# Second cross attention of a perceiver kernel: the two score passes one after the other, a quarter of the side matrix added by TensorE, value sums kept in a bank of PSUM

## The chip, the cores and the metric

The kernel runs on one core of a Trainium2 chip. The metric is the device time of one execution in microseconds; the time before is the median of three runs. The engines named here are TensorE (PE, with PEld for its weight loads), VectorE (DVE), ScalarE (ACT), GpSimd (POOL) and SyncE (SP). PSUM, which TensorE writes, has eight banks of 128 partitions by 512 float32.

## The reference, cut to what matters

A latent `x` of 128 rows by 256 passes through four layers. Each has a cross attention over a context of 12544 rows, a self-attention and a feed-forward part. The change is in the cross attention of the second layer (`l1x` in the kernel), with 16 heads of 16 features and a side matrix:

```python
K = (K_in @ Wk + bk).reshape(b, l, NH, DK).transpose(0, 2, 1, 3)
V = (V_in @ Wv + bv).reshape(b, l, NH, DK).transpose(0, 2, 1, 3)
Q = (Q_in @ Wq + bq).reshape(b, lp, NH, DK).transpose(0, 2, 1, 3)
KQ = jnp.einsum('bhld,bhpd->bhlp', K, Q) / np.float32(np.sqrt(DK))
KQ = KQ + mask_pad.reshape(b, 1, l, 1)
KQ = KQ + mask_attn.T.reshape(1, 1, l, lp)
alpha = jax.nn.softmax(KQ, axis=2)
O = jnp.einsum('bhlp,bhld->bhpd', alpha, V)
O = O.transpose(0, 2, 1, 3).reshape(b, lp, NH * DK)
return O @ Wo + bo
```

`K_in` and `V_in` are the context, `Q_in` the normalized latent, `mask_pad` a vector over the 12544 keys and `mask_attn` the side matrix, 128 by 12544. The softmax runs over the keys, with the same side matrix for all heads.

## The kernel before

**Stages.** The twelve parts run in order. Each cross attention needs keys and values of the whole context. These projections are cut into jobs (`project`, L199): for each of 25 chunks of 512 keys two key jobs (`K`, `k`, one for each half of the heads, L221) and two value jobs (`V`, `W`, L241), 99 for one attention. Each result goes to DRAM and is read back later. All jobs of all four attentions stand in one list, `self.jobs`, in order. They are taken from its head in three ways. `pump` in a cross attention's loop takes as many as `quota` says (L716); in the second attention one in three ticks of four. `one` (L155) takes one job ahead of every bank that a self-attention or feed-forward part asks for. `need` (L176) takes as many as it must until certain jobs are done, and so forces them where a load depends on them. A key job writes a staging tile `kst` of two parts, high and low, of which there are two buffers, and GpSimd's queue stores it; context chunks come through three buffers `ctx` on SyncE's queue.

**Two passes.** `cross` (L383) computes the scores twice. The first pass has queries on partitions and keys along the row, and finds the largest score of each query. The second pass has keys on partitions, 128 at a time, and queries of four heads along the row; it subtracts the maximum through an extra product, and its exponentials are the weights of the value product. Scores have a contraction of 32 rows (16 features in two parts, high and low), so four row tiles of TensorE work at once, each with a bank of its own. Four heads make a group (`G`), four groups one attention.

**Ticks.** A block is 2048 keys, 512 for each row tile; the last block has two row tiles of 128 keys. `ticks` (L446) holds for each group six blocks of four pieces and one short piece, 100 in all. The loop (L703) makes 127 turns: turn n runs the first pass of piece n and the second pass of piece n-27, because a group's second pass needs its maxima. So 27 turns hold first passes alone, 73 hold both, 27 hold second passes alone. The order of the instructions is written by hand (`manual_schedule`), and every engine runs its own list in that order.

**One turn.** `scores` (L587) takes two banks for the first pass of rows 2 and 3, four for the second pass and two more for the first pass of rows 0 and 1: all eight, from a ring of eight. It issues the products of both passes interleaved: rows 2 and 3 begin with the first pass while rows 0 and 1 begin with the second. VectorE then finds the maxima of rows 2 and 3 (`largest`, L553), adds the side matrix for the second pass (`exps`, L572) row by row, each followed by ScalarE's exponential, and finds the maxima of rows 0 and 1. In `largest` one instruction adds the side tile and takes the maximum (L562). Then the loop pumps a job, and `values` (L652) multiplies the exponentials of the turn before with the values into a new bank and VectorE adds that to an accumulator in SBUF (`acc`, L675).

**Loads.** `load_first(n+2)` (L461) and `load_second` (L481) issue their loads on SyncE's queue two turns ahead. The side tiles of the first pass (`f`, L475) are four for a block, from six buffers, so that two of a new block wait until two of the old are given back. The side tiles of the second pass (`ft`, L500) are one load of 256 KB for a piece, all four row tiles in it, from a transposed copy `fsideT`.

Of the kernel before, what the change touches and what calls it, by code (L numbers as in the profile page):

```python
# [10 lines left out]
F32 = mybir.dt.float32  # L11
# [8 lines left out]
P = 128  # L20
# [50 lines left out]
def _block(b):  # L71

    return (4, SEG) if b < NB - 1 else (2, P)
# [21 lines left out]
class Net:  # L95
    def __init__(self, ctx, tc, io):
# [7 lines left out]
        self.dp = ctx.enter_context(tc.tile_pool(name="scratch", bufs=1, space=DRAM))  # L104
        self.ps1 = ctx.enter_context(tc.tile_pool(name="ps1", bufs=8, space=PSUM))

# [55 lines left out]

    def bank(self, name):
        return self.ps1.tile([P, 512], F32, name=name, tag="one")

# [15 lines left out]
    def projections(self, names):  # L181
        self.kx, self.vx = {}, {}
        for l, name in enumerate(CROSS):
            if name not in names:
                continue
            gw = 17 * GROUP[name]
            for b in range(NB):
                ns, seg = _block(b)
                self.kx[name, b] = self.dp.tile([16, 32 * ns, seg], F32, name=f"{name}_kx{b}",
                                                tag=f"{name}_kx{b}")  # L190
                self.vx[name, b] = self.dp.tile([272 // gw, P, ns * seg // P, gw], F32,
                                                name=f"{name}_vx{b}", tag=f"{name}_vx{b}")
            if l == 0:
                passes = ["KVW", "k"]
            else:
                passes = ["KkVW"]
            self.project(name, passes)

    def project(self, name, passes):  # L199
# [183 lines left out]
    def cross(self, name, side=False, project=True, quota=None):  # L383
# [6 lines left out]
        with ExitStack() as es:  # L390
# [28 lines left out]
            def queries(g):  # L419

                q = qp.tile([P, 2, G, P], F32, name=f"{name}_q{g}", tag="q")
                qf = qp.tile([P, G, P], F32, name=f"{name}_qf{g}", tag="qf", bufs=1)
                wq = wqs.pop(g)
# [12 lines left out]

            kt, vt, ft, neg, qs, mxs, acc, wqs = {}, {}, {}, {}, {}, {}, {}, {}
            loaded = {"s": -1, "v": -1, "f": -1, "t": -1}
# [42 lines left out]
            def load_second(n):  # L481

                while loaded["v"] < min(n, len(ticks) - 1):
# [15 lines left out]
                    if side:  # L499
                        t = ep.tile([P, 4, P], F32, name=f"{name}_g{g}_{b}_{u}", tag="ft", bufs=3)  # L500
                        at = b * BK // P + u * 4
                        nc.sync.dma_start(out=t[:, :ns, :],
                                          in_=self.io["fsideT"][:, at : at + ns, :])
                        ft["t", g, b, u] = t

            def score_banks(n, kind, half):
# [4 lines left out]
            def first_ops(n, banks, t):  # L511
# [17 lines left out]
                return ops  # L529

            def second_ops(n, banks, t):

# [4 lines left out]
                for a in range(na):  # L537
                    at = (u * na + a) * P
                    for h in range(0, G, 2):
                        c = (a * G + h) * P  # L540
                        lhs = (mrow[r, b * SEG + at : b * SEG + at + P] if masked
                               else self.units[r, :])
                        ops.append((banks[t][:, c : c + 2 * P], r32(lhs),
                                    r32(neg[g][r, h : h + 2].rearrange("p h q -> p (h q)")),
                                    True, False))
                        for i in range(2):
# [25 lines left out]
            def exps(n, e, banks):  # L572
# [3 lines left out]
                for t, bank in banks.items():  # L576
                    src = bank[:, :m]
                    if side:
                        nc.vector.tensor_tensor(  # L579
                            out=e[:, t, :m].rearrange("p (h q) -> p h q", h=G),  # L580
                            in0=src.rearrange("p (h q) -> p h q", h=G),
                            in1=ft["t", g, b, u][:, t, :].unsqueeze(1).to_broadcast([P, G, P]),
                            op=ALU.add)
                        src = e[:, t, :m]
                    nc.scalar.activation(e[:, t, :m], src, AF.Exp)  # L585

            def scores(n, m):  # L587
# [37 lines left out]
                return (m, e) if second else None  # L625

            def lower(g):

# [23 lines left out]
            def values(part):  # L652
# [4 lines left out]
                na = min(4 // G, seg // P)  # L657
                ps = self.bank(f"{name}_av{n}")
                for t in range(ns):
                    for a in range(na):  # L660
                        for h in range(G):
# [3 lines left out]
                                             vt[g, b][:, at : at + 32],  # L665
                                             e[:, t, c * P : (c + 1) * P], start=(t == 0),
                                             stop=(t == ns - 1), skip_group_check=True)
                used = 32 * na * G
                first = b == 0 and u == 0
                if first:  # L670
                    acc[g] = self.small.tile([P, P], F32, name=f"{name}_acc{g}", tag="acc")
                if first:
                    nc.vector.tensor_copy(acc[g], ps[:, :P])
# [25 lines left out]
            pending = None  # L699
            load_queries(0)  # L700
            with tc.manual_schedule():
                qs[0] = queries(0)
                for n in range(len(ticks) + lag):  # L703
                    load_first(n + 2)
                    if n >= lag - 2:
                        load_second(n - lag + 2)
                    new = scores(n if n < len(ticks) else None, n - lag if n >= lag else None)
                    if n < len(ticks) and n % per == per - 1:
# [5 lines left out]
                    if n % per == 2 * per // 3 and n // per + 1 < 16 // G:  # L714
                        qs[n // per + 1] = queries(n // per + 1)
                    self.pump(quota(n, len(ticks), lag))  # L716
                    if n >= lag:
# [5 lines left out]
                values(pending)  # L723
                finish(16 // G - 1)

            nc.vector.tensor_tensor(out=o, in0=o, in1=self.row(f"{name}_vb"), op=ALU.add)
# [885 lines left out]
```

## Time and profile before

| What | us |
|---|---|
| Median of three runs (2648.64 to 2659.61) | 2657.65 |
| Profiled execution | 2661.88 |
| Its span, first to last instruction | 2660.1 |
| TensorE busy (matmul) | 2412.7 (91%) |
| VectorE busy | 1719.1 (65%) |
| ScalarE busy | 1229.3 (46%) |
| GpSimd busy | 419.6 (16%) |
| First score product of the second attention | 770.1 |
| First product of its second pass | 938.8 |
| Last first-pass product | 1361.8 |
| Last value product | 1471.4 |
| L562, add and maximum, 416 times | 254.3 busy |
| L579, side matrix added for the second pass, 392 times | 243.3 busy |
| L585, the exponentials of it, 392 times | 234.0 busy |
| L675, sums of the values, 96 times | 27.1 busy |

The page gives for each engine its busy time, a strip of 40 equal slices with the busy share in tenths, and groups of instructions by line. A group's line has the engine, the operation, output and inputs by the program's names with shapes, the number, then busy time, mean duration in ns, and the idle time of the engine just before, with what ended it. A line with "us, times, longest" is a wait: who waited for whom. In a timeline the columns are start, duration, engine, line, operation, output and inputs, and the number of instructions drawn together. Matmuls are pipelined, so a busy TensorE is not TensorE at its peak: the distance between starts says more.

### The profile page before, as it was taken

How to read it: one execution, taken by the hardware profiler on the slowest of the kernel's cores; microseconds unless marked ns; L12 is line 12 of the kernel's file. 1: busy time of each engine (PE TensorE's matmuls, PEld its weight loads, DVE VectorE, ACT ScalarE, POOL GpSimd, SP SyncE). 2: the span in 40 equal slices, each digit the busy share in tenths (PEclk: the TensorE clock that was granted, in tenths of full speed). 3: DMA queues.
4: the chain of work that ended last, by engine and by line, in shares of the span. 5: the costliest groups of instructions: out<-in, count | busy, mean ns of one | idle time of the engine just before them, and what ended most of it. 6: DMA issues, size and time to landing. Idle time of an engine off the chain costs nothing. (4 is left out here: it accounts for less than half of the span.)

```text
span 2660.1 us, 94232 instructions
## 1 busy us (share of the span) xinstructions
PE 2412.7 (91%) x41075; PEld 1874.3 (70%) x41075; DVE 1719.1 (65%) x3814; ACT 1229.3 (46%) x2256; POOL 419.6 (16%) x803
## 2 busy tenths in 40 slices
PE   7789989999968799999999898799999949999969
PEld 5567668886745577677677665478888737888858
DVE  1247668834134599989887753398887358888731
ACT  2225546663312145444457334446666532666642
POOL 3321110003322311111111332210000221000001
PEclk9889999999978889989899999899999967999979
DMA  8887774418967798877778676674343563444315
GB/s 277 246 260 216 226 215 135 134 53 287 296 195 215 232 323 276 298 251 256 274 246 274 188 205 196 198 238 137 115 137 95 155 193 100 136 119 135 102 49 208
DMA packets 256707, 524.56 MB, mean 197 GB/s; under 512 B 55692, under 2 KB 71510, under 8 KB 252326
## 3 DMA queue, kind: packets, MB, share of 16 engines
q1 hardware_dynamic: 175488, 309.75, 35.1%
q0 software_dynamic: 79312, 206.56, 26.6%
q8 instruction: 323, 5.29, 0.8%
q10 hardware_dynamic: 1494, 2.23, 0.2%
q14 instruction: 90, 0.74, 0.1%
HBM read 360.41 MB, written 157.79 MB: 195 GB/s over the span
## 5 line engine op out<-in xcount | busy, mean ns | idle before, releaser
L585 ACT ACTIVATE l1x_e<-l1x_e 128x512 f32<-128x512 f32 x392 | 234.0, 632 | 243.8 <-DVE l1x_e L579 243.8
L562 DVE CUSTOM_DVE_ANT_0 l1x_j<-l1x_s,l1x_f 128x512 f32<-128x512 f32 (+1 forms) x416 | 254.3, 655 | 55.3 <-DMA l1x_f<-in_fside 28.6
L567 DVE TENSOR_REDUCE l3x_mxs<-l3x_s 128x1 f32<-128x512 f32 (+1 forms) x400 | 244.1, 673 | 58.3 <-PE l3x_s L613 58.2
L567 DVE TENSOR_REDUCE l2x_mxs<-l2x_s 128x1 f32<-128x512 f32 (+1 forms) x400 | 249.2, 675 | 43.1 <-PE l2x_s L613 37.3
L567 DVE TENSOR_REDUCE l0x_mxs<-l0x_s 128x1 f32<-128x512 f32 (+1 forms) x400 | 244.3, 673 | 49.4 <-PE l0x_s L613 49.1
L585 ACT ACTIVATE l0x_e<-l0x_t 128x512 f32<-128x512 f32 (+1 forms) x400 | 203.9, 593 | 127.5 <-PE l0x_t L613 122.7
L585 ACT ACTIVATE l3x_e<-l3x_t 128x512 f32<-128x512 f32 (+1 forms) x400 | 203.8, 593 | 114.0 <-PE l3x_t L613 110.2
L585 ACT ACTIVATE l2x_e<-l2x_t 128x512 f32<-128x512 f32 (+1 forms) x400 | 203.5, 594 | 112.9 <-PE l2x_t L613 112.9
L579 DVE TENSOR_TENSOR l1x_e<-l1x_t,l1x_g 128x512 f32<-128x512 f32 x392 | 243.3, 683 | 11.2 <-PE l1x_t L613 10.0
L613 PE MATMUL l1x_t<-l1x_q,l1x_t 32*128 32x128 f32 x3136 | 174.0, 268 | 3.9 <-DMA l1x_t<-l1x_kx 3.6
L613 PE MATMUL l3x_t<-l3x_q,l3x_s 32*128 32x128 f32 x3136 | 171.3, 260 | 0.0
L613 PE MATMUL l0x_t<-l0x_q,l0x_s 32*128 32x128 f32 x3136 | 168.5, 259 | 3.0 <-issue 3.0
L613 PE MATMUL l2x_t<-l2x_q,l2x_s 32*128 32x128 f32 x3136 | 165.2, 262 | 0.0
L613 PEld LDWEIGHTS l3x_t<-l3x_q,l3x_s 32*128 32x128 f32 x3136 | 164.0, 189 | 0.0
L613 PE MATMUL l1x_s<-l1x_mrow,l1x_cq 32*128 32x256 f32 (+1 forms) x800 | 136.1, 333 | 30.1 <-DVE l1x_mxs L562 14.7
L613 PEld LDWEIGHTS l0x_t<-l0x_q,l0x_s 32*128 32x128 f32 x3136 | 161.0, 186 | 3.3 <-issue 3.3
L613 PEld LDWEIGHTS l1x_t<-l1x_q,l1x_t 32*128 32x128 f32 x3136 | 157.5, 190 | 6.9 <-DMA l1x_t<-l1x_kx 6.8
L613 PE MATMUL l1x_s<-l1x_s,l1x_q 32*128 32x256 f32 (+1 forms) x1600 | 150.8, 298 | 6.1 <-DMA l1x_s<-l1x_kx 5.9
L613 PE MATMUL l0x_s<-l0x_s,l0x_q 32*128 32x256 f32 (+1 forms) x1600 | 149.9, 289 | 6.2 <-DMA l0x_s<-l0x_kx 6.2
L613 PE MATMUL l2x_s<-l2x_s,l2x_q 32*128 32x256 f32 (+1 forms) x1600 | 150.4, 308 | 3.8 <-DMA l2x_s<-l2x_kx 3.5
L613 PEld LDWEIGHTS l2x_t<-l2x_q,l2x_s 32*128 32x128 f32 x3136 | 153.5, 186 | 0.0
L613 PE MATMUL l3x_s<-l3x_s,l3x_q 32*128 32x256 f32 (+1 forms) x1600 | 152.1, 289 | 0.2 <-issue 0.2
(668 smaller groups left out, 5788.0 us busy)
## 6 DMA issues: line engine op xcount, KB each, us to landing
l0x_c<-in_ctxT SPq DMA_DIRECT2D x48, 512.0 KB
l0x_kx<-l0x_ks POOLq DMA_DIRECT2D x96, 256.0 KB, 7.8
l0x_s<-l0x_kx SPq DMA_DIRECT2D x96, 256.0 KB
l1x_kx<-l1x_ks POOLq DMA_DIRECT2D x96, 256.0 KB, 6.7
l1x_s<-l1x_kx SPq DMA_DIRECT2D x96, 256.0 KB
l1x_f<-in_fside SPq DMA_DIRECT2D x96, 256.0 KB
l2x_kx<-l2x_ks POOLq DMA_DIRECT2D x96, 256.0 KB, 6.2
l1x_t<-l1x_kx SPq DMA_DIRECT2D x96, 256.0 KB
```

What stands on the lines that cost most here:

```text
L562: nc.vector.tensor_tensor_reduce(out=junk[:, :seg], in0=bank[:, j * seg : (j + 1) * seg], in1=ft[g, b][t][:, :seg], scale=1.0, scalar=-3.0e38,
L567: nc.vector.tensor_reduce(out=out, in_=bank[:, : len(hs) * seg].rearrange("p (h k) -> p h k", h=len(hs)), axis=AX.X, op=ALU.max)
L579: nc.vector.tensor_tensor(out=e[:, t, :m].rearrange("p (h q) -> p h q", h=G), in0=src.rearrange("p (h q) -> p h q", h=G), in1=ft["t", g, b ...
L585: nc.scalar.activation(e[:, t, :m], src, AF.Exp)
L613: nc.tensor.matmul(out, lhs, rhs, start=start, stop=stop, skip_group_check=True)
```

## The change

Only the second attention works differently; the ring of banks is rearranged for all.

- **Banks.** The ring `ps1` has seven banks and `ps2` one. Outside the second attention `bank` hands out the eighth in every eighth turn, so that it is a ring of eight as before. In the second attention only the seven are handed out.
- **Value sums.** In the second attention the eighth bank holds the value sums of a whole group. `values` accumulates in it over 25 pieces; VectorE copies it to `acc` once, after the last.
- **Passes in turn.** `scores_side` takes the place of `scores`: the first pass of all four row tiles, then their maxima in the order 0 to 3, then the pumped job, then the second pass of all four, then the exponentials.
- **Side matrix of row tile 0.** In the second pass it is added by TensorE: two products of the identity with the high and the low part of the side tile, over all 128 rows and 512 columns (the same 128 columns four times). They open the accumulation in that bank. VectorE adds the other three row tiles as before.
- **The two parts.** Seven new jobs, one for each block, stand in the list ahead of the second attention's projections. Each loads the block's side tiles of row tile 0, ScalarE makes the rounded part, VectorE the rest, and GpSimd's queue stores both in DRAM. They use a `ctx` and a `kst` buffer. A piece then loads its two parts (128 KB) and the other three side tiles (192 KB).
- **Room.** The unscaled queries of a group (`qf`) lie in a buffer of the tag `junk`.

```diff
     def bank(self, name):
+        if not self.seven:
+            self.turn += 1
+            if self.turn % 8 == 0:
+                return self.ps2.tile([P, 512], F32, name=name, tag="two")
         return self.ps1.tile([P, 512], F32, name=name, tag="one")
...
+            if name == "l1x":
+                self.side_parts()
             self.project(name, passes)
+
+    def side_parts(self):
...
+                f = self.bp.tile([P, 2, SEG], F32, name=f"fp_{b}", tag="ctx", bufs=3)
+                f = f[:, 0, :].rearrange("p (a k) -> p a k", a=4)
+                at = b * BK // P
+                nc.sync.dma_start(
+                    out=f[:, :n, :],
+                    in_=self.io["fsideT"][:, at : at + n * ns, :].rearrange(
+                        "p (a t) k -> p a t k", t=ns)[:, :, 0, :])
+                h = self.bp.tile([P, 2, SEG], F32, name=f"fh_{b}", tag="kst")
+                h = h.rearrange("p i (a k) -> p a i k", a=4)
+                nc.scalar.copy(r32(h[:, :n, 0, :]), f[:, :n, :])
+                nc.vector.tensor_tensor(out=r32(h[:, :n, 1, :]), in0=f[:, :n, :],
+                                        in1=h[:, :n, 0, :], op=ALU.subtract)
+                for i in range(2):
+                    nc.gpsimd.dma_start(out=self.fparts[:, 4 * b : 4 * b + n, i],
+                                        in_=h[:, :n, i])
+            self.jobs.append((("side", b), job))
...
-                        t = ep.tile([P, 4, P], F32, name=f"{name}_g{g}_{b}_{u}", tag="ft", bufs=3)
+                        t = ep.tile([P, 3, P], F32, name=f"{name}_g{g}_{b}_{u}", tag="ft", bufs=3)
+                        h = ep.tile([P, 2, P], F32, name=f"{name}_h{g}_{b}_{u}", tag="fh", bufs=3)
                         at = b * BK // P + u * 4
-                        nc.sync.dma_start(out=t[:, :ns, :],
-                                          in_=self.io["fsideT"][:, at : at + ns, :])
+                        nc.sync.dma_start(out=h, in_=self.fparts[:, 4 * b + u])
+                        nc.sync.dma_start(out=t[:, : ns - 1, :],
+                                          in_=self.io["fsideT"][:, at + 1 : at + ns, :])
...
+            def side_ops(n, banks):
+
+                g, b, u = ticks[n]
+                for i in range(2):
+                    part = ft["h", g, b, u][:, i, :].unsqueeze(1).to_broadcast([P, G, P])
+                    nc.tensor.matmul(banks[0], r32(ident), r32(part), start=(i == 0), stop=False,
+                                     skip_group_check=True)
...
+            def scores_side(n, m, pieces):
+
+                if n is not None:
...
+                    banks = score_banks(n, "s", range(4))
+                    row_tiles([first_ops(n, banks, t) for t in banks])
+                    largest(n, banks)
+                pieces()
+                if m is None:
+                    return None
+                banks = score_banks(m, "t", range(4))
+                side_ops(m, banks)
+                row_tiles([second_ops(m, banks, t) for t in banks])
+                e = ep.tile([P, 4, SEG], F32, name=f"{name}_e{m}", tag="e")
+                exps(m, e, banks)
+                return m, e
...
+                if side:
+                    if first:
+                        avs[g] = self.ps2.tile([P, 512], F32, name=f"{name}_av{g}", tag="two")
+                    ps = avs[g]
+                else:
+                    ps = self.bank(f"{name}_av{n}")
...
                                              vt[g, b][:, at : at + 32],
-                                             e[:, t, c * P : (c + 1) * P], start=(t == 0),
-                                             stop=(t == ns - 1), skip_group_check=True)
+                                             e[:, t, c * P : (c + 1) * P],
+                                             start=(t == 0 and (first or not side)),
+                                             stop=(t == ns - 1 and (last or not side)),
+                                             skip_group_check=True)
                 used = 32 * na * G
-                first = b == 0 and u == 0
-                if first:
+                if side and not last:
+                    return
+                if first or side:
                     acc[g] = self.small.tile([P, P], F32, name=f"{name}_acc{g}", tag="acc")
```

`row_tiles` issues the row tiles' products in turn, one of each row. In `exps` only row tiles 1 to 3 are added by VectorE, and `second_ops` opens no new accumulation in row tile 0.

## The prediction

> **What bounds the kernel now.** I read the forty slices first, then the second attention (names beginning `l1x`) cut into its three stages, then one tick of it on VectorE and on TensorE, and last who waits for the side loads. A tick is one turn of the hand-written loop: the first pass of piece n beside the second pass of piece n-27.
>
> ```profile
> PE   7789989999968799999999898799999949999969
> DVE  1247668834134599989887753398887358888731
> ```
>
> A slice is 66.5 us. Slices 11 to 22 are the second attention. From slice 14 to 20 VectorE and TensorE are both at 7 to 9 tenths, so it must be told which one really sets the pace. The next view gives busy time by stage: first passes alone (27 ticks), both passes (73 ticks), second passes alone (27 ticks).
>
> ```profile
> core 0: us, PE busy (x) PEld busy (x) DVE busy (x) ACT busy (x) POOL busy (x), PEclk, DMA share, GB/s
> 770.00:938.50 168.50, 134.93 (x944) 90.54 (x944) 83.88 (x250) 28.27 (x46) 41.10 (x65) 0.84 0.72 219
> 938.50:1362.50 424.00, 402.18 (x7255) 304.61 (x7258) 391.63 (x1002) 203.23 (x344) 48.35 (x90) 0.94 0.81 276
> 1362.50:1472.00 109.50, 107.09 (x2061) 80.40 (x2053) 81.08 (x168) 75.30 (x129) 18.33 (x32) 0.98 0.78 247
> ```
>
> In the middle stage VectorE is busy 391.6 of 424 us: 92%, the bound. In the last it has 28 us to spare and TensorE is busy 98%: there TensorE is the bound. One VectorE tick:
>
> ```profile
> 1200.20 0.28 DVE L675 TENSOR_TENSOR l1x_acc<-l1x_acc,l1x_av 128x128 f32<-128x128 f32 x1
> 1200.40 0.69 DVE L562 CUSTOM_DVE_ANT_0 l1x_j<-l1x_s,l1x_f 128x512 f32<-128x512 f32 x1
> 1201.01 0.09 DVE L562 DVE_READ_ACCUMULATOR2_ANT l1x_mxs<- 128x1 f32 x1
> ...
> 1201.62 2.48 DVE L579 TENSOR_TENSOR l1x_e<-l1x_t,l1x_g 128x512 f32<-128x512 f32 x4
> 1204.02 0.68 DVE L562 CUSTOM_DVE_ANT_0 l1x_j<-l1x_s,l1x_f 128x512 f32<-128x512 f32 x1
> ...
> 1205.23 0.28 DVE L675 TENSOR_TENSOR l1x_acc<-l1x_acc,l1x_av 128x128 f32<-128x128 f32 x1
> ```
>
> Starts count, not durations, since instructions overlap: the sum 0.20, a maximum 0.61, four adds 2.40, a tick 5.03 us. TensorE's pieces, where nothing holds them:
>
> ```profile
> 779.22 0.39 PE L613 MATMUL l1x_s<-l1x_mrow,l1x_cq 32*128 32x256 f32 x4
> ...
> 780.13 1.98 PE L343 MATMUL l1x_k<-l1x_c,l1x_kw 128*128 128x512 f32 x4
> ...
> 1406.23 0.39 PE L613 MATMUL l1x_t<-l1x_ng,l1x_mrow 32*128 32x256 f32 x4
> ...
> 1407.51 1.99 PE L343 MATMUL l2x_v<-l2x_vw,l2x_c 128*128 128x256 f32 x8
> 1409.44 1.08 PE L664 MATMUL l1x_av<-l1x_e,l1x_v 128*32 128x128 f32 x32
> 1410.45 0.39 PE L613 MATMUL l1x_t<-l1x_ng,l1x_mrow 32*128 32x256 f32 x4
> ```
>
> First pass alone 0.91, second pass alone 1.28, a projection job 1.93, the value product 1.01 us, each with its drain to the next kind. Last, two waits, the first in the first stage, the second in the middle one:
>
> ```profile
> DVE l1x_j L562 <- DMA l1x_f<-in_fside: 22.7, 7, 5.1
> SPq L478 <- DVE l1x_mxs L562: 139.3, 37, 12.4
> ```
>
> Before, the maxima of row tiles 2 and 3 come first and those of 0 and 1 last. The side tiles of a new block for rows 2 and 3 go into the buffers that the old block's rows 0 and 1 give back. So SyncE's queue stands until the end of a tick, and VectorE wants just these tiles first: 3.2 us a time.
>
> **Part by part.** *VectorE* loses the sum (0.20) and one add of four (0.60): 5.03 becomes 4.23 us (the sum now grows in a bank of its own, with one copy of 0.28 a group, four in all), with 0.67 more where a key job is pumped (1216.33 to 1217.00 in the trace).
>
> *TensorE, two side products a tick.* A product of the 128x128 identity with 512 reduced columns stands nowhere in the trace. Lower bound 0.215, half of the 0.43 that one record of the key job takes for 512 columns (four records, 1.72); upper bound that 0.43. Nearest is a 32x256 reduced product: rounds of four row tiles start every 0.117 us, so 512 columns need at most 0.23. I take 0.225, a pair 0.45, and keep 0.86 for the range. The identity's first weight load (0.11, the step of the four 128x128 products of L644) hides behind a job, and shows where there is none. The Trainium skill, FP8 and Floating Point Precision, section TensorE Precision Notes, counts four passes for a true FP32 product and has a reduced form; a true product of 512 columns is two records here, 0.86 us, so one pass would be 0.215 and a pair 0.43, 2 us less in the sum than my value. No run here shows it yet.
>
> *TensorE, passes in turn.* Interleaved, both passes took 2.04 us (1156.13 to 1158.17); apart 0.91 + 1.28 = 2.19. Job and side products are of one form, so the drain is paid once. With a job: 0.91 + 1.93 + 0.45 + 1.28 + 1.01 = 5.58 us. Without: 0.91 + 0.45 + 0.31 (weights, drain) + 1.28 + 1.01 = 3.96, below VectorE's 4.23. **So TensorE becomes the bound in three ticks of four**, as a job is pumped in three of four.
>
> *Middle stage.* Of 73 ticks 5 are short. 51 x 5.58 + 17 x 4.23 = 356; five short ones at about 5 (one takes 6.7 now, with 0.6 idle and 0.8 that goes) 25; two queries at 1.8 of TensorE 4: 385. Idle of VectorE now is 424 - 392 = 32; of it the waits for the side tiles (5.9) and of the sum for the value product (9.8) go, and I let 16 stand: 401, **-23 us**. Bounds: all 32 stays and 15 more (+8), or none (-39).
>
> *Seven banks for eight.* In a job tick the next first pass wants the bank of second-pass row 0. The second pass ends 4.57 us into the tick, ACT reads that bank 0.63 us without VectorE, so it is free near 5.4, wanted at 5.58. Nothing, but with 0.2 to spare; were row 0 still added by VectorE, 0.6 a tick would show.
>
> *Order 0 to 3.* The side tiles of rows 2 and 3 now are asked for after the first two maxima and wanted after two others: 1.22 + 0.91 gained of 3.2, so 15 of 22.7: **-15** (0 to -23).
>
> *Last stage.* TensorE bound: 21 x 0.45 + 6 x 0.76 = **+14** (to +26 at the upper bound). VectorE's relief is worth nothing here.
>
> *Seven side jobs.* They stand ahead of this attention's projections: one in the tick near 381, six in the six calls of the first self-attention. At 381 TensorE now waits 6.7 us for projection weights: gone there, -7. In the self-attention (23 us) six jobs of 1.93 leave, but each side job takes one of two staging buffers whose stores land 6.7 us after the issue; the first ACT copy that finds none free stops VectorE's queue behind it, evictions included. Six jobs over two buffers are about 24 us against 23, and the weights' wait comes behind them: +3 (-5 to +8). Seven projection jobs move into the first stage, where they are forced: 7 x 1.93 = +13.5. Together **+9.5** (-1 to +21). SyncE gets seven issues, POOL's queue fourteen of 0.6 us.
>
> *Loads.* One more issue a tick on SyncE's queue (0.33), with 320 KB for 256, ahead of the adds' tile; behind it stand the next keys. A late side tile would hold the two products and with them the second pass, the value product and the next first pass on TensorE. Prefetch is two ticks, 11 us. Taken as hidden; the price without cover is a rival.
>
> Sum: -23 - 15 + 14 + 9.5 = **-14.5 us**. The profiled execution took 2661.9 (span 2660.1), 4.2 above the median 2657.65; against the median: **2643 us**.
>
> **Rivals.** *The side pair at the price of a full-precision record* (0.86): job ticks 5.99, others 4.35, so 51 x 0.41 + 17 x 0.12 + 27 x 0.41 = 34 more: +19.5, **2677**, slower. For it: no row shows a reduced product on the whole array. Against it: the 0.23 of the 32-row ones. It decides from a pair of about 0.8 on; at 0.64 the gain is nil.
>
> *Transfers become the bound.* DMA is busy 0.81 x 424 = 343 us in the middle stage. The second pass's side loads are 8960 of 50776 packets of a queue that takes 62.5%: 47 us. Two packets for one cost 12 (by bytes) to 47 more (by packets): 355 to 390 of 401. At the upper end keys come late, the middle stage keeps its 424 less some 4: **2662**. For it: the two microseconds after 936, when this stage's first tiles come, are already full (share above 1). Against it: packets of 1 and 1.5 KB are not small. The skill, DMA: Bandwidth & Descriptors, section Why small descriptors are slow, has some 3 cycles a packet of bus overhead, which at 1 KB is a tenth: that would be near the lower end, and no rival.
>
> *All stalls go*: middle -39, side tiles -23, last +14, side jobs -1: **2609**. Against it: keys still arrive by DMA just in time.
>
> *The side matrix isn't moved off the path*: excluded, since VectorE's count is fixed by the code.
>
> **Chances.** Forecast 0.48 (own range 2628 to 2656; 0.33 of it faster, 0.15 within), all stalls gone 0.08, transfers 0.16 (0.12 within, 0.04 slower), dear pair 0.28 (slower). Within 0.5% (13 us) is what this kernel's measurement cannot tell from no change. So faster 0.41, same 0.27, slower 0.32. The range runs from 2609 to 2690: the dear pair with the side jobs' upper bound is 2677 + 12.
>
> **What would show it.** Right: in the middle stage VectorE busy about 330 us and TensorE's idle near nothing; side products starting 0.21 to 0.23 us apart; ticks with a job 5.5 to 5.7 us; the last stage longer by 14; the wait for side tiles below 10; the stall near 381 gone and the first stage's projections more by seven. Wrong: first passes waiting for banks, the granted clock below 0.9 in the middle stage, key loads as the commonest releaser of TensorE.

## The result and the profile after

The changed kernel took 2690.0 us (median of 4, 2682.3 to 2691.0) against 2654.5 us before on the same chip: ratio 1.0128, 95% interval 1.0097 to 1.0159. It is slower by 1.3%, where 2643 us had been forecast.

Cut at the same points as before (first and last start of the `l1x_s` and `l1x_t` products), the two profiled executions compare like this, in us:

| stretch | before | after | difference | forecast |
|---|---|---|---|---|
| start to the first first pass of l1x | 770.2 | 771.7 | +1.5 | -4 |
| first stage (first passes alone) | 168.6 | 194.9 | **+26.3** | -1.5 |
| middle stage (both passes) | 423.0 | 408.9 | -14.1 | -23 |
| last stage (second passes alone) | 106.2 | 118.0 | +11.8 | +14 |
| all that follows | 1192.1 | 1195.4 | +3.3 | 0 |
| span | 2660.1 | 2688.9 | +28.8 | -14.5 |

The slices of the changed kernel (67.2 us each), then its three stages:

```profile
PE   7889979998978899999999898799999959999969
...
DVE  1247657844143478788865663388888358888731
```

```profile
core 0: us, PE busy (x) PEld busy (x) DVE busy (x) ACT busy (x) POOL busy (x), PEclk, DMA share, GB/s
771.70:966.60 194.90, 159.07 (x1010) 105.79 (x1009) 90.68 (x261) 33.94 (x55) 47.93 (x76) 0.83 0.73 224
966.60:1375.50 408.90, 391.51 (x7318) 298.78 (x7318) 337.06 (x853) 207.95 (x341) 47.78 (x90) 0.97 0.88 293
1375.50:1493.50 118.00, 118.00 (x2123) 88.59 (x2119) 60.50 (x113) 78.36 (x129) 17.40 (x31) 1.00 0.79 247
```

VectorE's digits in slices 15 to 20 (counted from 0) went from 8 or 9 to between 6 and 8. In the middle stage it is busy 337 of 409 us, and TensorE 391.5: the bound has moved as forecast. But the first stage, which should have shrunk a little, is longer by 26 us. A middle tick with a job, on TensorE:

```profile
1205.96 0.39 PE L681 MATMUL l1x_s<-l1x_mrow,l1x_cq 32*128 32x256 f32 x4
...
1206.88 1.98 PE L376 MATMUL l2x_k<-l2x_c,l2x_kw 128*128 128x512 f32 x4
1208.30 1.03 PE L576 MATMUL l1x_t<-l1x_h,l1x_id 128*128 128x512 f32 x2
1209.27 0.39 PE L681 MATMUL l1x_t<-l1x_ng,l1x_mrow 32*128 32x256 f32 x4
...
1210.55 1.08 PE L748 MATMUL l1x_av<-l1x_e,l1x_v 128*32 128x128 f32 x32
...
1211.56 0.39 PE L681 MATMUL l1x_s<-l1x_mrow,l1x_cq 32*128 32x256 f32 x4
```

From 1205.96 to 1211.56 it is 5.60 us (forecast 5.58). Job and pair together take 2.39 (1206.88 to 1209.27; forecast 1.93 + 0.45). The pair alone is drawn at 0.97 (1208.30 to 1209.27), beside a job of 1.42, so only their sum can be compared; what one product costs is measured below (e12). The tick is as it was worked out; what is not in it are the waits. In the first stage (first three lines) and the middle stage (last two), with the sum, the number of times and the longest:

```profile
PE l1x_s L681 <- DMA l1x_s<-l1x_kx: 13.3, 5, 4.7
...
DVE l1x_j L610 <- DMA l1x_f<-in_fside: 17.7, 8, 3.9
...
SPq L249 <- PE l1x_v L376: 77.4, 11, 10.3
...
PE l1x_t L576 <- DMA l1x_h<-fparts: 10.3, 8, 3.6
...
SPq L515 <- DVE l1x_mxs L610: 87.3, 36, 7.5
```

The chunks' line in the first stage before:

```profile
SPq L216 <- PE l1x_v L343: 42.6, 6, 9.0
```

In the first stage SyncE's queue now stands 77 us at the context chunks of forced projections (L249; 42.6 before), and TensorE waits 13.3 us for keys that are loaded behind them. In the middle stage the queue stands at the first pass's side tiles (L515), and the side parts, issued behind, come late.

### The profile page after: what moved, and what is told of

Same layout as the page of the kernel before. It is cut to its first block, busy times and chain, and to the rows that moved or that the text cites. A ratio compares the mean times of both kernels' runs of the same rounds, so it can differ in the third digit from the quotient of the medians.

```text
span 2688.9 us, 94645 instructions
## 1 busy us (share of the span) xinstructions
PE 2439.0 (91%) x41275; PEld 1894.2 (70%) x41275; DVE 1653.5 (61%) x3625; ACT 1242.6 (46%) x2263; POOL 428.1 (16%) x817
## 5 line engine op out<-in xcount | busy, mean ns | idle before, releaser
L627 DVE TENSOR_TENSOR l1x_e<-l1x_t,l1x_g 128x512 f32<-128x512 f32 x292 | 183.8, 684 | 92.8 <-PE l1x_t L681 55.0
L633 ACT ACTIVATE l1x_e<-l1x_e 128x512 f32<-128x512 f32 x292 | 177.8, 631 | 17.9 <-DVE l1x_e L627 12.7
L661 PE MATMUL l3x_s<-l3x_mrow,l3x_cq 32*128 32x256 f32 (+1 forms) x800 | 137.8, 329 | 15.1 <-DMA l3x_mrow<-l3x_row 13.0
L661 PE MATMUL l0x_s<-l0x_mrow,l0x_cq 32*128 32x256 f32 (+1 forms) x800 | 134.2, 325 | 16.0 <-DVE l0x_ks L264 8.9
L661 PE MATMUL l2x_t<-l2x_ng,units 32*128 32x256 f32 x784 | 133.9, 350 | 1.8
L661 PEld LDWEIGHTS l0x_s<-l0x_s,l0x_q 32*128 32x128 f32 x1600 | 125.8, 195 | 8.8 <-DMA l0x_s<-l0x_kx 8.8
```

Source lines behind the costliest of these rows:

```text
L627: nc.vector.tensor_tensor(out=e[:, t, :m].rearrange("p (h q) -> p h q", h=G), in0=src.rearrange("p (h q) -> p h q", h=G), in1=ft["t", g, b ...
L661: nc.tensor.matmul(out, lhs, rhs, start=start, stop=stop, skip_group_check=True)
```

## The experiments

Sixteen variants ran, each against the kernel before on the same chip. Its median moved between 2658 and 2662 us from one group of runs to the next, so ratios are compared. Stages are in us of one profiled execution; two executions of nearly the same code differ by some 5 in a stage. The variants also moved stretches that they do not touch: among kernels without side jobs the first attention took 375 to 389 us from its first to its last second pass.

| run | first | middle | last | median | ratio to before (95%) |
|---|---|---|---|---|---|
| e1_side_late | 194.0 | 406.7 | 118.1 | 2666.4 | 1.0008 (0.9983-1.0034) |
| e2_before_side_jobs | 190.2 | 427.0 | 106.2 | 2688.6 | 1.0097 (1.0064-1.0130) |
| e3_turn_only | 178.4 | 397.1 | 107.5 | 2632.6 | 0.9895 (0.9854-0.9936) |
| e4_old_maxima | 190.2 | 411.5 | 118.0 | 2690.4 | 1.0097 (1.0066-1.0128) |
| e5_turn_old_maxima | 180.2 | 401.8 | 107.4 | 2637.3 | 0.9891 (0.9855-0.9928) |
| e6_turn_vector_sum | 176.0 | 391.7 | 107.2 | 2637.1 | 0.9877 (0.9844-0.9911) |
| e7_more_quota | 170.9 | 414.6 | 118.0 | 2654.8 | 0.9968 (0.9936-1.0000) |
| e8_turn_eight_f | 166.2 | 428.1 | 108.3 | 2658.6 | 0.9976 (0.9949-1.0003) |
| e9_turn_quota | 160.4 | 394.1 | 107.3 | 2642.4 | 0.9938 (0.9915-0.9960) |
| e10_turn_f8_k13 | 154.6 | 386.4 | 107.9 | 2611.4 | 0.9833 (0.9787-0.9879) |
| e11_turn_quota_f8 | 143.8 | 387.4 | 107.2 | 2621.0 | 0.9850 (0.9800-0.9900) |
| e12_one_side_product | 191.5 | 407.0 | 111.7 | 2676.0 | 1.0058 (1.0023-1.0094) |
| e13_quota_f8 | 159.8 | 384.4 | 118.0 | 2618.3 | 0.9838 (0.9807-0.9870) |
| e14_second_first | 195.3 | 440.1 | 118.0 | 2718.7 | 1.0215 (1.0142-1.0288) |
| e15_before_f8 | 150.1 | 408.6 | 106.1 | 2616.3 | 0.9831 (0.9801-0.9861) |
| e16_pair_while_first | 160.5 | 391.2 | 108.8 | 2609.4 | 0.9789 (0.9740-0.9838) |

**Is it the place of the side jobs?** e2 puts them alone into the kernel before:

```diff
+            if name == "l1x":
+                self.side_parts()
             self.project(name, passes)
```

> The kernel before with nothing but the seven side jobs in front of the projections; what they write is read by nobody. Theory A: first stage 20 to 27 us longer than before (190 to 196), total 2675 to 2682. Theory B: first stage within 6 us of the 168.6 before, total 2650 to 2660.

First stage +21.6, total +26 us (0.97%): theory A. Nothing reads what these jobs write; the jobs alone, at this place in the list, cost 26 of the 35 us that the changed kernel lost on the whole. Counted by products, 48 projection jobs of this attention fall into the first stage in place of 41, in e2 as in the changed kernel.

e1 moves the jobs behind the projections in the changed kernel, from tick 19 on:

```diff
-            if name == "l1x":
-                self.side_parts()
             self.project(name, passes)
+            if name == "l1x":
+                self.side_parts()
...
+                    if side and 19 <= n < 18 + NB:
+                        self.need([("side", n - 18)])
```

> The changed kernel with the seven side jobs behind the second attention's projections (one or two a tick from tick 19 on, their loads two jobs ahead) instead of in front of them. Theory A (the side jobs in front push seven projection jobs into the first stage, where they are forced as a burst, and the chunk loads that they bring stand before the key loads): first stage, from the first l1x_s product to the first side product, 165 to 175 us instead of 195, total 20 to 27 us below the changed kernel, 2663 to 2670. Theory B (the first stage is slowed by what the change does there itself: the order of the maxima, the ring of seven banks, the passes in turn): first stage still 188 us or more, total within 6 us of the changed kernel.

The total fits theory A (2666), the stage doesn't (194): 41 projection jobs are in it again, but the side jobs stand there themselves. ScalarE waits 9.0 us for their staging buffers, VectorE 11.4 for ScalarE's part of them, and the first chunk of the next attention comes 15.8 us late behind them. The gain lies elsewhere (the second attention starts 7.7 us earlier, the part behind it is 10.6 shorter), for a reason that no run isolates. So e1 settles nothing alone. e7 undoes the push instead, by more jobs in the first attention. The expectation says seven; the rule takes two ticks of three, so it is six, and 42 projection jobs are left in the first stage:

```diff
-            "l0x": lambda n, m, lag: int(n % 3 > 0) if 14 <= n < 54 else 0,
+            "l0x": lambda n, m, lag: int(n % 3 > 0) if 14 <= n < 64 else 0,
```

> The changed kernel with a longer quota in the first attention (until tick 64 instead of 54: seven jobs more), so that the seven side jobs push no projection job into the second attention's first stage. If the pushed jobs are what lengthens that stage: 165 to 180 us instead of 195, the first attention up to 13 longer, total 2665 to 2682. If the stage is slow for another reason (side loads, passes in turn, banks): 188 us or more, total 2685 or more.

170.9 us: the pushed jobs are what lengthened the stage. The total fell further than expected, by 1.6 points of the ratio, since the first attention also ended 22 us earlier (its last second pass started at 579.5, in the changed kernel at 601.5). The traces show a reason. In the changed kernel the seven side jobs run close together in the first attention (386 to 410 us), and ScalarE, which also makes that attention's exponentials, stands there until a staging buffer (`fh`) is stored to DRAM (`fparts`). Its wait, and one of TensorE's behind it, from 374 to 420:

```profile
ACT fh L224 <- DMA fparts<-fh: 13.6, 4, 7.0
PE l0x_t L661 <- ACT l0x_e L633: 5.0, 1, 5.0
```

TensorE's waits there sum to 17.9 us (6.7 in the kernel before, for projection weights). With e7's quota the side jobs stand in the ticks, at most one in each (382 to 417 us): no wait for a staging buffer is left, and TensorE waits 2.7. So e7 removes two costs of the side jobs, the push and this bunch. e9 is the control, the same quota with no side work at all (on e6, below):

> The kernel of e6_turn_vector_sum (passes in turn alone) with the longer quota of e7 in the first attention. It is the control for e7: there are no side jobs here that could be the cause. If a projection job in the first stage costs the 3 us that e2 showed (21.6 for seven), seven fewer forced jobs there: first stage 152 to 162 us (e6: 176), total 2612 to 2622. If the quota is worth all of the 35 us that it brought the changed kernel for a reason of its own in the first attention: total 2605 or less. If it only undoes the push: first stage 170 or more, total 2630 to 2642.

The first stage shrank by 15.6 as worked out (35 projection jobs in place of 41, so 2.6 us each), yet the total didn't gain (0.9938 against 0.9877). The quota has no gain of its own; in e7 it mends what the side jobs had done.

**The order of the maxima.** e4 is the changed kernel, e5 is e3 (below), each with rows 2, 3, 0, 1 again:

```diff
-                    largest(n, banks)
+                    largest(n, {t: banks[t] for t in (2, 3, 0, 1) if t in banks})
```

> The changed kernel with the maxima of the first pass in the order before (rows 2, 3, 0, 1). If the order from 0 to 3 is worth what I gave it: first stage 10 to 20 us longer than the changed kernel's 195.5, total 2700 to 2710. If the wait for the side tiles is only one of two that end together (key loads the other): first stage within 4 us of it, total 2686 to 2694.

> The kernel of e3_turn_only (no side jobs, no side products, passes in turn) with the maxima in the order before, rows 2, 3, 0, 1. If the order from 0 to 3 only moves the wait from the side tiles to the key loads that stand behind them on SyncE's queue, or costs a little: first stage 166 to 178 us (e3: 178.4, before: 168.6), total 2622 to 2640. If the order is worth the 15 us I gave it: first stage 188 or more, total 2645 or more.

Neither total moved (1.0097 beside 1.0128, 0.9891 beside 0.9895). The waits tell why. The first stage of e5, old order, TensorE's and VectorE's waits:

```profile
PE l1x_s L676 <- DVE l1x_mxs L605: 16.0, 15, 4.7
...
DVE l1x_j L605 <- DMA l1x_f<-in_fside: 23.4, 7, 5.3
```

The same of e3, order 0 to 3:

```profile
PE l1x_s L676 <- DMA l1x_s<-l1x_kx: 16.3, 5, 6.9
...
DVE l1x_j L605 <- DMA l1x_f<-in_fside: 16.8, 7, 4.2
```

VectorE's wait for side tiles falls by 6.6 us, and TensorE waits as long as before: 16 us for banks that VectorE gives back late in the one, 16 us for keys in the other. Both stand behind the same point of SyncE's queue, as e10 below shows: with two more buffers there, order 0 to 3, VectorE waits 2.0 us for tiles and TensorE 3.1 for keys.

**Which part of the change pays?** e3 has no side jobs and no side products (VectorE adds all four rows); e6 has, beside, the value sum on VectorE each tick and eight banks in one ring, so that of the change only the passes in turn (with the pumped job between them) and the order are left.

```diff
-                side_ops(m, banks)
...
-                    if side and t:
+                    if side:
```

and e6 on top of it

```diff
-                if side:
-                    if first:
-                        avs[g] = self.ps2.tile([P, 512], F32, name=f"{name}_av{g}", tag="two")
...
+                ps = self.bank(f"{name}_av{n}")
...
-            self.seven = side
+            self.seven = False
```

> The changed kernel without side jobs and side products: VectorE adds the side matrix to all four row tiles again; passes in turn, maxima from row 0 to 3, seven banks and the value sum in a bank of its own stay. Theory A: first stage at or below before's 168.6 (my step said 15 less: 154), last stage 106 as before, middle stage 400 to 415 (a job tick is TensorE's 5.13 us or VectorE's 4.83), total 2620 to 2645. Theory B: first stage 188 or more, total 2655 or more.

> The kernel of e3_turn_only with the value sum added by VectorE in every tick again and all eight banks in one ring: of the change, the passes in turn and the order of the maxima are left. If the gain of e3 (some 30 us on before) comes from VectorE's 0.20 us a tick: middle stage 408 to 415 (e3: 397, before: 423), total 2643 to 2652. If it comes from the passes in turn, which let VectorE start its adds without waiting for the first pass: middle stage 396 to 402, total 2628 to 2638.

Both are faster than before by over 1%. The passes in turn bring it, since the order is worth nothing (e5) and the value sum's bank adds nothing (e6); whether the job's place between them has a part in it was not run. The middle stage of e6, columns as above:

```profile
core 0: us, PE busy (x) PEld busy (x) DVE busy (x) ACT busy (x) POOL busy (x), PEclk, DMA share, GB/s
946.70:1338.40 391.70, 374.02 (x7185) 283.57 (x7180) 384.23 (x994) 205.11 (x341) 48.21 (x90) 0.99 0.87 294
```

VectorE has the work of before, but is busy 98% instead of 92%: 7.5 us of its 32 idle are left. e12 takes one product of the pair away in the changed kernel:

```diff
-                for i in range(2):
+                for i in range(1):
```

> The changed kernel with one side product a tick instead of two: the low part of the side matrix of row tile 0 is left out of the second pass (its load stays). If TensorE sets the pace in the 51 middle ticks with a job and in all 27 of the last stage, and a product costs 0.215 us: middle stage 396 to 400 us (changed kernel: 409), last stage 111 to 113 (118), first stage as it is, total 2670 to 2676. If the transfers or the key loads set the pace of the middle stage: middle 405 to 410, last 112, total 2680 to 2688.

Last stage -6.3, so 0.23 us a product over 27 ticks. The middle gave 2 of the 11 us: TensorE's wait for the side parts rose from 10.3 to 16.5. That is what the expectation named as the other case: loads hold what the product gives up.

**SyncE's stand.** e8 gives the first pass eight side tiles instead of six, so that the queue need not wait for the maxima of the block before.

```diff
-                                        bufs=6)
+                                        bufs=8)
```

> The kernel of e3_turn_only with eight buffers for the side tiles of the first pass instead of six (one instead of two for the maxima's unused output, to make room), so that SyncE's queue need not stand until the old block's first two maxima. If that stand is what makes both side tiles and keys late: first stage 148 to 162 us, middle stage 385 to 397, total 2600 to 2620. If the first stage is bound by the forced projection jobs and their chunk loads instead: first stage 170 to 180 us, total 2625 to 2638.

The first stage shrank, but the middle grew by 31 us. To make room, the buffer for the maxima's unused output had been cut from two to one, and VectorE's instructions show its price:

```profile
1100.43 0.69 DVE L606 CUSTOM_DVE_ANT_0 l1x_j<-l1x_s,l1x_f 128x512 f32<-128x512 f32 x1
1101.05 0.08 DVE L606 DVE_READ_ACCUMULATOR2_ANT l1x_mxs<- 128x1 f32 x1
1101.27 0.69 DVE L606 CUSTOM_DVE_ANT_0 l1x_j<-l1x_s,l1x_f 128x512 f32<-128x512 f32 x1
```

Maxima start 0.84 us apart instead of 0.61, up to 0.9 us more a tick. e10 makes the room with 13 key buffers instead of 14 (on e6), e11 adds e7's quota:

```diff
-            kp = es.enter_context(tc.tile_pool(name=f"{name}_k", bufs=22 if keep else 14))
+            kp = es.enter_context(tc.tile_pool(name=f"{name}_k", bufs=22 if keep else 13))
```

> The kernel of e6_turn_vector_sum with eight buffers for the first pass's side tiles (13 instead of 14 key buffers make the room; the maxima keep two buffers for their unused output, since with one they started 0.84 instead of 0.61 us apart in e8). If SyncE's stand at those buffers still costs: first stage 164 to 170 us (e6: 176), middle stage 380 to 388 (e6: 392), total 2615 to 2628. If the stages are bound by TensorE and VectorE themselves: first stage 172 or more, middle 389 or more, total 2632 to 2642.

> Both of e9 and e10 together. If their gains are of different waits and add: 2595 to 2612. If both go at the same wait (key loads behind SyncE's stand): no better than the better one of the two by more than 5 us.

e10 is 1.7% faster than before; e11's shorter first stage (143.8) is given back ahead of it, where the second attention starts 14.5 us later than in e10. e14 puts the second pass's loads ahead of the first's in the changed kernel:

```diff
-                    load_first(n + 2)
                     if n >= lag - 2:
                         load_second(n - lag + 2)
+                    load_first(n + 2)
```

> The changed kernel with the loads of the second pass (values, side parts, side tiles) issued ahead of those of the first pass (keys, side tiles) in each tick. If the side parts are late because they stand behind SyncE's stand at the first pass's side buffers: TensorE's wait for them in the middle stage below 3 us instead of 10.3, middle stage 396 to 402 (409), total 2676 to 2684 against the changed kernel's 2690. If the first pass's keys then come as late as the side parts did: their wait rises by as much and the middle stage stays at 405 or more.

Slower: the wait changed hands and grew. TensorE no longer waits for side parts, and in e14's middle stage for the keys:

```profile
PE l1x_s L681 <- DMA l1x_s<-l1x_kx: 30.2, 15, 5.0
```

e13 is the changed kernel with e7's quota and eight side tiles (12 key buffers); e15 the kernel before with the eight side tiles alone; e16 is e13 with the pair only in the 73 second passes that stand beside first passes; for the others the four rows of the side matrix go into a first-pass buffer, free by then:

```diff
+                        if loaded["v"] >= len(ticks) - lag:
+                            t = ep.tile([P, SEG], F32, name=f"{name}_g{g}_{b}_{u}", tag="f",
+                                        bufs=8)
...
-                side_ops(m, banks)
+                if ("h", *ticks[m]) in ft:
+                    side_ops(m, banks)
```

> The changed kernel with the longer quota of e7 and eight side buffers for the first pass (12 instead of 14 key buffers make the room). If what remains then is the side product's own price: compared with e11 (2621, the same without side work) the last stage 10 to 12 longer, the middle 10 to 14, total 2640 to 2650, slower than the passes in turn alone with eight buffers. If the side product pays once its loads are in time: total below 2621.

The middle stage of e13:

```profile
929.10:1313.50 384.40, 381.67 (x7318) 293.31 (x7318) 335.77 (x851) 207.30 (x340) 47.37 (x89) 1.00 0.93 312
...
PE l1x_t L576 <- DMA l1x_h<-fparts: 0.3, 1, 0.3
```

TensorE is busy 99%, the side parts are in time, and the stage takes 384 us, 24 less than in the changed kernel with the same products. With the loads in time the pair costs nothing in this stage beside e11's 387, and 10.8 in the last. It gains nothing either: without the pair VectorE is the bound (busy 383.7 of e11's 387.4 us), with it TensorE (381.7 of 384.4), and the two bounds lie that close. By the profiled spans e13 is the slower (2619.5 against 2605.3), by the ratios it isn't (0.9838 and 0.9850); whether the pair pays on the whole then stays open, and the 2640 expected was too much.

> The kernel before with eight buffers for the first pass's side tiles (12 instead of 14 key buffers make the room) and nothing else. If SyncE's stand alone held the kernel before: middle stage 395 to 400 us (423; VectorE's own work is 392), first stage 150 to 158 (168.6), total 2615 to 2625. If the interleaved passes hold the middle stage too: middle 410 to 420, first 150 to 158, total 2632 to 2645.

Two more buffers in the kernel before, and nothing of the change: 1.7% faster. The first stage is the shortest but one, and SyncE's stand in it falls from 69.7 us to 16.8:

```profile
SPq L478 <- DVE l1x_mxs L562: 69.7, 13, 16.8
...
SPq L478 <- DVE l1x_mxs L562: 16.8, 9, 8.7
```

VectorE's wait for side tiles falls with it from 22.7 to 6.1 us, and TensorE's for keys from 4.5 to 1.4. The middle keeps 17 us more than e6's, near the end that was expected if the interleaved passes hold it too; the total is lower than that end all the same, with the second attention starting at 757.4 instead of 770.2, which the buffers don't explain.

> The kernel of e13_quota_f8 with the side pair in the 73 second passes of the middle stage only; in the last stage, where TensorE sets the pace and VectorE has room, VectorE adds the side matrix to all four row tiles. Last stage 106 to 108 us instead of 118, the rest as in e13, total 2604 to 2611. If the gain is given back in what follows: 2614 to 2622.

The last stage fell to 108.8, close to the 106 to 108 worked out, and the total is the best, 0.9789; its interval overlaps those of e10, e11, e13 and e15, so that it beats those is not shown. All five beat both kernels.

## Why the prediction was wrong

**The step that failed is the first stage, and in it two terms.** Of the 43 us between the forecast -14.5 and the span's +28.8, the first stage holds 28, the middle stage 9 and the stretch ahead of the attention 5.5.

*"Order 0 to 3: -15" measured 0* (e4, e5). I followed the side tile that VectorE waits for and not what stands behind it on the same queue. With the new order the tiles come a little sooner, and the keys behind them are late in their place. Only more buffers shortened both waits (e10, e15).

*"Seven side jobs: +9.5" measured +26* (e2). That seven projection jobs would be forced was right, counted in e2 and in the changed kernel. Their price was wrong: 1.93 us each is the price in a busy stage, and in the first stage seven cost 21.6, 3.1 each. e2's first stage, columns as above:

```profile
770.30:960.50 190.20, 152.41 (x985) 101.75 (x985) 86.69 (x254) 32.53 (x53) 47.42 (x75) 0.85 0.75 221
```

TensorE is busy 17.5 us longer there than before (134.9), so 2.5 a job, and idle 4.2 us longer, 0.6 a job. The changed kernel shows both halves at work. One burst, TensorE and then SyncE's queue:

```profile
797.70 0.80 PE L681 MATMUL l1x_s<-l1x_s,l1x_q 32*128 32x256 f32 x8 [4.67 <-DMA l1x_s<-l1x_kx]
...
799.07 3.69 PE L376 MATMUL l1x_v<-l1x_vw,l1x_c 128*128 128x256 f32 x8
802.60 3.60 PE L376 MATMUL l1x_k<-l1x_c,l1x_kw 128*128 128x512 f32 x8
806.03 3.62 PE L376 MATMUL l1x_v<-l1x_vw,l1x_c 128*128 128x256 f32 x16
809.48 1.88 PE L376 MATMUL l1x_k<-l1x_c,l1x_kw 128*128 128x512 f32 x4
...
802.79 7.27 SPq L249 DMA_DIRECT2D l1x_c<-in_ctxT  x2
810.29 1.45 SPq L480 DMA_DIRECT2D l1x_s<-l1x_kx  x1
811.83 8.34 SPq L515 DMA_DIRECT2D l1x_f<-in_fside  x4
820.22 3.32 SPq L480 DMA_DIRECT2D l1x_s<-l1x_kx  x2
```

The burst itself is 12.2 us (799.07 to 811.29). SyncE stands for its chunks until 810, then issues a key and side tiles, stands again until 820, and only then loads the keys of the following ticks, which are late once more. And the first job, of the usual eight products, takes 3.5 us instead of 1.93. The busy time in four windows, columns as above (the third figure from the right is the granted clock), says why:

```profile
793.00:797.70 4.70, 0.03 (x3) 0.01 (x2) 1.19 (x3) 0.11 (x1) 0.00 (x0) 0.79 0.78 282
797.70:802.60 4.90, 4.90 (x29) 4.00 (x30) 2.67 (x10) 0.00 (x0) 0.00 (x0) 0.51 0.03 12
802.60:806.00 3.40, 3.40 (x9) 1.52 (x8) 0.75 (x1) 1.27 (x2) 1.31 (x2) 1.00 0.60 184
...
819.60:833.20 13.60, 11.16 (x62) 8.30 (x62) 6.68 (x22) 0.85 (x2) 0.00 (x0) 0.50 0.67 218
```

The clock fell within the wait of 4.7 us (0.79 over it; 1.00 up to 795.7, 0.50 from there), and TensorE ran 4.9 us more at 0.51, then at 1.00. Such a wait is paid a second time. The profile before had it in its clock of 0.84 for the first stage, and I didn't use it. The Trainium skill, TensorE: Matmul & The Clock Gate, section "HAM oscillation — how this bites in real kernels", warns of idle gaps of over some 3.4 us, after which TensorE runs at half its clock. This wait agrees with it, but the trace doesn't show 3.4 us to be the limit: from 819.6 the clock is at 0.50 again, where no wait of the 7 us before was over 2.0.

What stays open in this stage: without any side work it was 7 to 12 us longer than before, in either order of the maxima (e3 178.4, e5 180.2, e6 176.0 against 168.6). The forecast had nothing for that, and no run isolates what in the passes in turn does it.

*Middle stage, -23 forecast, -14 measured.* The tick was right to 0.02 us, and e13 shows the sum of TensorE's work (385 forecast, 384.4 in all). The 16 us that I let stand beside it were 24: I had taken them from VectorE's idle time, though TensorE was to be the bound. TensorE was idle for 17.4 us and, at a clock of 0.97, busy 9.8 longer than with the same products in e13 (391.5 against 381.7). Most of the idle time is there because "Taken as hidden", of the loads, was wrong: prefetch is two ticks, but the side parts stand behind a queue that stands up to 7.5 us at the first pass's tiles (10.3 us of TensorE's waits; 3.6 more are for keys). The rival of the transfers had the right place with the wrong cause; it was no lack of transfer rate, since e13 moved 312 GB/s where the changed kernel moved 293.

*Last stage, +14 forecast, +11.8 measured*: right, with 0.23 us a product (e12; 0.225 taken). The rival of the dear pair, 0.86, is excluded by the job tick. Its total of 2677 was nearer than the forecast, for a wrong reason; that the stated range ended at 2690, the measured median, is luck, since that end was made of the dear pair. *Seven banks for eight* cost nothing that showed: TensorE's waits for VectorE in the middle stage sum to 1.5 us. *Up to the second attention* -4 forecast, +1.5 measured: the first attention took 13.4 us more between its first and last second pass, the stretch up to the self-attention's scores gave 9 back. Six of the seven side jobs, forecast for the self-attention, ran with the first one at 386 to 410 us in the first attention. The wait of 6.7 us near 381 is gone as forecast, but the 17.9 us of waits behind the staging buffers stand in its place: that these would stop an engine was foreseen, where it happened was not.

Of the signs named beforehand, VectorE's busy time, the job tick, the last stage and the seven more projections came true. TensorE's idle time and the wait for side tiles (17.7 us) didn't, and key loads as TensorE's commonest releaser, in the first stage, were a sign of being wrong.

**What the sum hid.** It was made for the whole change against the kernel before. Taken part by part, its own numbers say that without the pair a job tick is 5.13, the others VectorE's 4.83, so the middle stage 389 instead of 401: the pair cost 12 there and 14 in the last stage, and all of the gain was the passes in turn. The changed kernel against e3 shows it (408.9 against 397.1 in the middle stage, 118.0 against 107.5 in the last); with the loads in time (e13) only the last stage's price is left.

Open stays why e1 gained behind the second attention, and why the first attention's time moves by ten or more us among variants without side jobs.

## What to carry to other kernels

Price each part of a change against the others as well as against before: here one part, the passes in turn, brought over 1%, and two more, the side jobs and the pair, spent it. When a queue stands at a buffer ring, list everything issued behind it; an order of work that shortens one of these waits only hands it to the next, whereas two more buffers in the kernel before (e15) brought 1.7%, at least as much as the passes in turn without them (e3, e6). Work that is forced into a stage with long waits costs its price at the clock that stage gets, plus what its loads push back.

## What the runs showed of the hardware

- The granted clock fell to half within a wait of 4.7 us and stayed there for 4.9 us of work (0.51 from 797.70 to 802.60), so that a projection job took 3.5 us instead of 1.93. It also fell where no wait was over 2.0 us (0.50 from 819.6 to 833.2).
- A product of a 128x128 matrix with 512 reduced columns cost 0.23 us (e12: 6.3 us in 27 ticks).
- VectorE's maxima started 0.61 us apart with two output buffers in turn, 0.84 with one (e8), though nothing reads that output.
